# Three of six pairs and three of four batch rows close in the last work unit instead of one unit ahead of it

## The chip, the cores and the metric

The kernel runs on one core of one Trainium2 chip. The metric is the device time of one execution in microseconds (us); lower is better. All arithmetic is in 32-bit floats.

## The reference, cut to what matters

For eight batch rows of 512 tokens with 256 features the reference computes a mixture of eight experts and a shared one, and adds the input:

```
g = einsum('bsd,edf->ebsf', x, Wg);  u = einsum('bsd,edf->ebsf', x, Wu)      # 8 experts, F = 1024
expert = einsum('be,ebsd->bsd', gates, einsum('ebsf,efd->ebsd', silu(g) * u, Wd))
shared = (silu(x @ Sg) * (x @ Su)) @ Sd
out = x + (1 - sg) * expert + sg * shared        # sg: one number for each batch row
```

The kernel treats the shared expert as a ninth, with its factor `sg`.

## The kernel before

**Units.** The nine experts, two groups of four 128-wide blocks of F, and two halves of the batch (four rows each) make 36 units, done one after another. In a unit, `i` is a block of F, `j` a batch row, and `h_[i, j]` is the 128x512 tile `silu(gate) * up * coefficient`. There are 16 of them. `gate_up` makes them; `down` multiplies the 16 tiles of a unit by the weights Wd while the next unit's `gate_up` runs. In the written order of a unit, G is one step of `gate_up`, D one step of `down`, X one step of `tail`.

**Pairs.** Off the diagonal, the tiles `h_[i, j]` and `h_[j, i]` are made as one of six pairs, `PAIRS = ((1, 0), (0, 2), (3, 0), (1, 2), (3, 1), (3, 2))`. For each pair and each of gate (m = 0) and up (m = 1), three products are made where four would be needed: `R1_step` (L537) makes one that both tiles share, and `R_step` (L547) one for each. VectorE (DVE) puts D on them (L542, L552), ScalarE (ACT) applies Silu (L477), DVE multiplies (L482). ACT copies a start value into each PSUM bank ahead of it (L532).

**Down.** The same device is used again: a pair costs three 128x512 products, `r` and `s` (or `S`, which is carried in a running sum) and one of `X = h_[j, i] - h_[i, j]` (L674). Each batch row then costs two, `q` on a sum over column tiles and `b` on a sum over row tiles. These feature sums, `rows` and `cols`, are made on GpSimd (POOL) one 128x512 addition at a time (L577), and the weight forms of a pair, `ad`, `a2`, `ud` and `wd`, on POOL too (L408 to L462). So 6 x 3 + 4 x 2 = 26 products replace the 32 that a plain product of 16 tiles with two halves of Wd would take.

**Running sums.** Over the units of a batch half the results gather in SBUF tiles `accb`, `accB`, `accV`, `accS`, written by `put`, `carried` and `seeded`. `closes(u)` says in which unit a pair's V and S sums are resolved into `accb` and `accB` of its two rows, with DVE operations L605, L603, L678 and L607. A row's product `b` starts from `accb` copied by ACT into its bank (L615), so it waits for the last pair of that row.

**The end before.** The second last unit (8_0) closes all pairs and rows. The last unit (8_1) has no pairs below: `tail` makes 16 tiles x two token halves, each two 128x256 products in place of one 128x512 (L770). The closed sums are turned on DVE (L739), stored to a DRAM tile in 128-byte pieces (`endrows`, L953, eight stores a row), loaded back in row order (`endin`, L757, two loads a row), added to x on POOL (L761), and last a DVE addition puts the tail on (L779) and a store writes the output (L781). All these stores and loads are on SyncE's queue (SP), in its written order.

**What sets the order.** TensorE (PE) and POOL run in the order in which the program text records them (`manual_schedule`); the other queues get an order from a scheduler, with `issue_after` adding order where it is written. Every engine works in its own order, so an instruction that waits holds all behind it on its engine.

Of the kernel before, what the change touches and what calls it, by code (L numbers as in the profile page):

```python
# [17 lines left out]
def kernel(  # L18
# [46 lines left out]
    CI = (0.0, 1.0, -1.0, 2.0)  # L65
    PAIRS = ((1, 0), (0, 2), (3, 0), (1, 2), (3, 1), (3, 2))

    OWN = (0, 1, 2, 3)
# [405 lines left out]
    def finish(u, m, i, j, bank):  # L474
        if m == 0:
            s = spool.tile([P, S], F32, tag="sg", name=f"sg{i}{j}_{u.name}")
            nc.scalar.activation(s, bank, AF.Silu)  # L477
            u.sg[i, j] = s
        else:
            b = NI * u.h + j  # L480
            t = hpool.tile([P, S], F32, tag="h", name=f"h{i}{j}_{u.name}")
            made = ve.scalar_tensor_tensor(  # L482
                t, u.sg[i, j], coef[:, u.e, b : b + 1], bank, ALU.mult, ALU.mult
            )
            if i == j:
                first_order(u, made, "h", i)
            u.h_[i, j] = t
# [68 lines left out]
    def h_sums(u, p):  # L556


        i, j = PAIRS[p]
        if u.n + 1 == len(units):  # L560
            return
        u.X[p] = tpool.tile([P, S], F32, tag="t", name=f"X{p}_{u.name}")
        made = (gp if closes(u) and p in (1, 2, 3, 4) else ve).tensor_tensor(  # L563
            u.X[p], u.h_[j, i], u.h_[i, j], ALU.subtract
        )
        first_order(u, made, "X", p)
        for k, l in ((i, j), (j, i)):
            for which, n in (("rows", k), ("cols", l)):
                u.sums.append((which, n, (k, l)))
# [12 lines left out]

    def closes(u):

        return u.n + (2 if u.h + 1 == NH else 1) == len(units) * (u.h + 1) // NH

    def down(u, acc):
# [54 lines left out]
        def pair(p):  # L642
# [8 lines left out]
            def second():  # L651
                args = u.Wd[p][j], u.h_[j, i]
                if p in OWN and not closes(u):
                    carried(("S", p), *args)
                    return
                if p in OWN:
                    o, full = seeded(("S", p), *args)
                    if not full:
                        ve.tensor_add(o, o, acc["S", p])
                else:  # L660
                    o, _ = single(("s", p), *args)
                put(("B", i), o, -1.0)
                put(("V", p), o, -1.0)

            if closes(u) and p < SWAPPED:
                second()
                yield
                A, k = first()
            else:
                A, k = first()  # L670
                yield
                second()
# [3 lines left out]
            )  # L676
            if closes(u):
                ve.tensor_add(A, A, acc["V", p])  # L678
                put(("b", i), A, 1.0 / d)
                put(("b", j), A, -1.0 / d)  # L680
            else:
                put(("V", p), A, 1.0)
# [4 lines left out]
        done = {}  # L687
        for what in (0, 1, 2, 3, 4, "p0", "q0", 5, "q1", "p1", "q2", "p2", "q3", "p3"):
            if isinstance(what, int):
# [14 lines left out]
            else:  # L704
# [3 lines left out]
                done[what] = po  # L708
            if closes(u) and f"p{i}" in done and f"q{i}" in done:
                if CI[i] != 0.0:  # L710
                    put(("B", i), done[f"p{i}"], -CI[i])
                for r in (0, 1):
                    ends[u.h, i, r] = acc["bB"[r], i]
# [4 lines left out]
    def turn_back(h, i, r):  # L718

        if i not in backs:  # L720
            backs[i] = iopool.tile([P, S // 32, 2, 32], F32, tag="io", name=f"to{h}_{i}")
        t = backs[i]
        ve.transpose(t[:, :, r], ends.pop((h, i, r)).rearrange("p (c d) -> p c d", d=32))
        if (i, 1 - r) not in BACK[BACK.index((i, r)):]:
            for q in range(4):
                outgoing.append((squares(out, NI * h + i, q), t[ts(q, 32)]))

    last_rows = {}
    tails = {}
    ended = {}  # L730
    end_rows = {}

    def end_step(kind, i):

        b = NI * (NH - 1) + i
        if kind == "turn":
            t = iopool.tile([P, 2, S], F32, tag="io", name=f"end{i}")
            for r in range(2):
                ve.transpose(t[:, r], ends.pop((NH - 1, i, r)))  # L739
            ended[i] = t  # L740
        elif kind == "store":
            to = end_rows[i] = dram.tile([S, D], F32, tag=f"end{i}", name=f"endrows{i}")
            at = to.rearrange("(c r t) d -> r t c d", r=32, t=NT)
            for r in range(2):
                for q in range(4):
                    outgoing.append((
                        at[:, :, :, ts(4 * r + q, 32)],
                        ended[i][ts(q, 32), r].rearrange("r (t c d) -> r t c d", t=NT, d=32),
                    ))
        elif kind == "x":  # L750
            last_rows[i] = load_rows(xpool, "x", b)
        elif kind == "load":
            at = end_rows[i].rearrange("(p t) d -> p t d", t=NT)
            end_rows[i] = []
            for c in range(2):
                t = sumpool.tile([P, 2, D], F32, tag="sum", name=f"endin{i}_{c}")
                nc.sync.dma_start(t, at[:, 2 * c : 2 * c + 2])  # L757
                end_rows[i].append(t)
# [4 lines left out]
    def tail(u, i, j, c):  # L763

        first = (j, c) not in tails
        if first:
            pool, tag = (ps_g, f"g{c}") if j == 2 else (ps_o, f"po{c}")
            tails[j, c] = pool.tile([P, 2, D], F32, tag=tag, name=f"tail{j}_{c}")
# [6 lines left out]
    def store_rows(j, c):  # L775
        b = NI * (NH - 1) + j
        xr = last_rows[j][c]
        for t in (0, 1) if j == NI - 1 and c == 1 else (slice(0, 2),):
            ve.tensor_add(xr[:, t], tails[j, c][:, t], xr[:, t])  # L779
            at = out[b].rearrange("(p c t) d -> p c t d", c=2, t=2)[:, c]  # L780
            nc.sync.dma_start(at[:, t], xr[:, t])  # L781

# [8 lines left out]
    def gate_up(u, nxt):  # L791
# [5 lines left out]
        def sums(p):  # L797
            x_sums(u, p)
            w_sums(u, p)

        for p, make in ((0, w_difference), (0, w_sums), (1, w_difference), (1, w_sums)):
            make(u, p)
        if u.n:
            make_at(u, 3)
        w_difference(u, 2)
        ahead = ((0, x_difference), (0, x_sums), (1, x_difference), (1, x_sums), (2, x_difference))
        if u.n:
# [3 lines left out]
        for kind, i, m in hub_steps(u):  # L811
# [17 lines left out]
            at = range(10, 16) if u.n in LATE_FORMS else range(3, 14, 2)  # L829
            if step == at[0] - 1 and u.n and nxt is not None:  # L830
                make_ad(u)
            if step in at and u.n and nxt is not None:
                d_forms(u, at.index(step))
            yield
        if u.n == 0:
            make_ad(u)
            for p in range(len(PAIRS)):
                d_forms(u, p)
        for p in range(len(PAIRS)):
            last = p + 1 == len(PAIRS)  # L840
            if p + 3 < len(PAIRS):
                (differences if u.n else partial(w_difference, u))(p + 3)
            if nxt is not None:
                if p >= 2:
                    load_w(nxt, p - 2)
                    if p < 5:
                        make_at(nxt, p - 2)
            store_forms(u)
            if p == 5 and nxt is not None:
                load_d(nxt)  # L850
            if not last and u.n:
                seed(u, p + 1)
            for m in range(2):
                if not last and (u.n or p or m):
                    R1_step(u, p + 1, m)
                elif last and nxt is not None:
# [3 lines left out]
                for r in range(2):  # L860
                    R_step(u, p, m, r)
                    if m == 1 and r == 1:
                        h_sums(u, p)
                        if u.n == 0 and p + 2 < len(PAIRS):
                            seed(u, p + 2)
                        if p + 2 < len(PAIRS):
                            sums(p + 2)
                        if u.n == 0 and p < 2:
# [8 lines left out]
    FIRST = "TGGTGGTGG" + "G" * 16 + BLOCK * 5  # L877
    LAST = HUB + BLOCK + "GGXGGXGGX" * 5 + "X" * 17
    TAILS = [
        tuple(int(n) for n in what)  # L880
        for what in (
            "000 100 001 101 200 201 300 301 110 111 010 011 210 211 310 311 "
            "220 020 120 221 021 121 330 030 130 331 031 131 320 321 230 231"
        ).split()
    ]
    END_STEPS = {
        7: (("turn", 0), ("store", 0)), 16: (("turn", 1), ("store", 1)), 18: (("x", 0),),
        20: (("turn", 2), ("store", 2), ("x", 1)), 22: (("load", 0), ("x", 2)),
        24: (("turn", 3), ("store", 3), ("x", 3)), 28: (("add", 0),), 30: (("load", 1),),
        34: (("add", 1),), 37: (("load", 2),), 40: (("add", 2),), 44: (("load", 3),),  # L890
        47: (("add", 3),),
    }

    for i in range(NI):
# [37 lines left out]
    for u in units:  # L932
# [6 lines left out]
        for what in FIRST if u.n == 0 else LAST if nxt is None else ORDER:  # L939
            if what == "G":  # L940
                if nG == TAKE:
                    for _ in behind:
                        pass
                    if u.opens:
                        acc = {}
                    behind = down(u, acc) if nxt is not None else iter(())
                if final and nxt is not None and nG in (18, 21, 24, 27):
                    load_x(u.h + 1, (nG - 18) // 3)
                if nxt is None:
                    for what_, i in END_STEPS.get(nG, ()):  # L950
                        end_step(what_, i)
                if outgoing:
                    nc.sync.dma_start(*outgoing.pop(0))  # L953
                if nG > TAKE and nG % 2 == 0 and u.sums:
                    add_sum(u)
# [5 lines left out]
            elif what == "T":  # L961
                for _ in range(2):
                    next(turning, None)
            elif what == "X":
                i, j, c = TAILS.pop(0)
                tail(u, i, j, c)
# [56 lines left out]
```

## Time and profile before

| what | us |
|---|---|
| time, median of three runs (lowest, highest) | 2434.99 (2433.91, 2435.68) |
| the profiled execution's own time | 2433.26 |
| its span, first to last instruction | 2431.5 |
| PE busy, share of the span | 2425.3 (100%) |
| POOL busy | 2085.3 (86%) |
| DVE busy | 1918.3 (79%) |
| ACT busy | 1240.0 (51%) |
| mean granted TensorE clock | 1.000 of full speed |

A row of the timeline gives the start, the duration, the engine, the program line, the operation, out<-in, and in brackets the idle time ahead of it with what ended it. A 128x512 product shows as two records; from the start of one product to the next takes 0.86 us, and two token halves of a tail step (x2 records of 128x256 each, four in all) take the same 0.86 us. That is called a slot in what follows. 2431.5 is a span; 1.8 us lie around it in the profiled execution.

### The profile page before, as it was taken

Reading aid. Unit: us, or ns where it says so; the run is one execution under the profiler, and the core shown is the slowest. Engines: PE = TensorE matmul, PEld = TensorE weight load, DVE = VectorE, ACT = ScalarE, POOL = GpSimd, SP = SyncE. Lnnn points to the kernel's source line nnn. Section 1 sums busy time; section 2 is a strip of 40 time slices with the busy share of each in tenths; the row PEclk is TensorE's granted clock in tenths of the full one; section 3 lists DMA queues with packets and bytes.
Section 4 is the critical chain, followed back from the end, with each engine's and each line's share of the span. In section 5 each row is a group of like instructions: output and inputs, shape, how many; then the busy total and the mean of one; then the engine's idle time right before and its main releaser. Section 6 shows DMA issues by size and latency. Waiting matters only on the chain.

```text
span 2431.5 us, 22779 instructions
## 1 busy us (share of the span) xinstructions
PE 2425.3 (100%) x5736; PEld 1085.0 (45%) x5736; DVE 1918.3 (79%) x2861; ACT 1240.0 (51%) x2294; POOL 2085.3 (86%) x2321
## 2 busy tenths in 40 slices
PE   9999999999999999999999999999999999999999
PEld 4444444444444444444444444444444444444446
DVE  7788878778787877787887777777877777777795
ACT  5555454554555555555455555555455555555542
POOL 8988888898988989898888888888888888888882
PEclk9999999999999999999999999999999999999999
DMA  4333333334333333334353323323333333233245
GB/s 150 114 110 111 107 95 103 119 117 125 105 120 105 101 113 94 109 113 124 119 122 112 91 83 91 92 87 90 100 104 104 95 99 91 87 89 93 83 133 140
DMA packets 221201, 257.92 MB, mean 106 GB/s; under 512 B 64016, under 2 KB 156432, under 8 KB 221072
## 3 DMA queue, kind: packets, MB, share of 16 engines
q1 hardware_dynamic: 220240, 256.17, 35.7%
q8 instruction: 48, 0.79, 0.1%
q14 instruction: 81, 0.66, 0.1%
q10 hardware_dynamic: 832, 0.30, 0.0%
HBM read 238.59 MB, written 17.83 MB: 105 GB/s over the span
## 4 chain that ended last, share of the span: by engine, by line
PE 99%; DVE 1%; issue 0%; ACT 0%; DVEq 0%
PE c L547 30%; PE c L537 15%; PE c L515 10%; PE c L493 10%; PE r L639 7%; PE r L674 7%; PE b L616 5%; PE S L616 5%; PE q L639 5%; PE s L639 2%; PE tail L770 1%; PE B L616 0%; DVE h L482 0%; DVE c L542 0%; DVE c L552 0%
## 5 line engine op out<-in xcount | busy, mean ns | idle before, releaser
L547 PE MATMUL c<-b,wb 128*128 128x512 f32 x1728 | 847.2, 592 | 0.0
L477 ACT ACTIVATE sg<-c 128x512 f32<-128x512 f32 x576 | 343.8, 597 | 574.4 <-DVE c L552 332.4
L482 DVE SCALAR_TENSOR_TENSOR h<-sg,coef,c 128x512 f32<-128x512 f32 x576 | 427.4, 742 | 242.2 <-PE c L547 134.8
L547 PEld LDWEIGHTS c<-b,wb 128*128 128x128 f32 x1728 | 328.2, 190 | 409.2 <-issue 388.7
L537 PE MATMUL c<-v,u 128*128 128x512 f32 x864 | 441.1, 593 | 0.8 <-ACT c L532 0.8
L577 POOL TENSOR_TENSOR rows<-rows,h 128x512 f32<-128x512 f32 x280 | 369.3, 1319 | 0.0
L542 DVE TENSOR_TENSOR c<-D,c 128x512 f32<-128x512 f32 x432 | 298.7, 692 | 78.1 <-ACT sg L477 59.3
L577 POOL TENSOR_TENSOR cols<-cols,h 128x512 f32<-128x512 f32 x280 | 358.4, 1280 | 0.0
L552 DVE TENSOR_TENSOR c<-c,D 128x512 f32<-128x512 f32 x432 | 298.5, 691 | 21.2 <-PE c L547 20.7
L493 PE MATMUL c<-x,w 128*128 128x512 f32 x572 | 274.5, 592 | 0.0
L429 POOL TENSOR_TENSOR wb<-u,wb 128x256 f32<-128x256 f32 x108 | 78.8, 730 | 221.4 <-ACT wb L427 221.4
L537 PEld LDWEIGHTS c<-v,u 128*128 128x128 f32 x864 | 163.4, 190 | 207.9 <-issue 167.7
L674 PE MATMUL r<-X,ud 128*128 128x512 f32 x420 | 214.5, 592 | 0.0
L639 PE MATMUL r<-h,wd 128*128 128x512 f32 x420 | 214.5, 592 | 0.0
L515 PE MATMUL c<-x,at 128*128 128x512 f32 x432 | 208.5, 592 | 0.0
L525 ACT COPY D<-c 128x512 f32<-128x512 f32 x284 | 165.7, 584 | 81.4 <-DVE h L482 81.3
L563 DVE TENSOR_TENSOR X<-h,h 128x512 f32<-128x512 f32 x202 | 198.1, 981 | 6.8
L577 POOL TENSOR_TENSOR rows<-h,h 128x512 f32<-128x512 f32 x140 | 195.1, 1394 | 0.0
L577 POOL TENSOR_TENSOR cols<-h,h 128x512 f32<-128x512 f32 x140 | 180.6, 1290 | 0.0
L499 ACT COPY P<-c 128x512 f32<-128x512 f32 x216 | 126.4, 587 | 106.1 <-PE c L493 101.5
L493 PEld LDWEIGHTS c<-x,w 128*128 128x128 f32 x572 | 108.5, 190 | 135.9 <-issue 111.7
L615 ACT COPY S<-accS 128x512 f32<-128x512 f32 x132 | 77.8, 590 | 157.5 <-DVE accV L603 140.7
(115 smaller groups left out, 3473.6 us busy)
## 6 DMA issues: line engine op xcount, KB each, us to landing
b<-xs SPq DMA_DIRECT2D x210, 512.0 KB, 3.6
v<-xs SPq DMA_DIRECT2D x210, 256.0 KB, 2.6
wd<-in_L_cond_Wd_dram SPq DMA_DIRECT2D x32, 512.0 KB, 4.9
w<-in_L_cond_Wg_dram SPq DMA_DIRECT2D x127, 128.0 KB, 3.5
w<-in_L_cond_Wu_dram SPq DMA_DIRECT2D x127, 128.0 KB, 3.6
f<-xd SPq DMA_DIRECT2D x12, 512.0 KB, 5.2
xs<-f SPq DMA_DIRECT2D x18, 256.0 KB, 2.9
xin<-in_x_dram SPq DMA_DIRECT2D x16, 256.0 KB, 4.4
```

The source lines that it names most:

```text
L477: nc.scalar.activation(s, bank, AF.Silu)
L482: made = ve.scalar_tensor_tensor(t, u.sg[i, j], coef[:, u.e, b : b + 1], bank, ALU.mult, ALU.mult)
L493: nc.tensor.matmul(bank, u.raw[i][:, m, 0], xhub[u.h, i][:, 0], start=True, stop=True)
L515: nc.tensor.matmul(bank, u.at[i][:, m], xhub[u.h, i][:, 1], start=False, stop=True, skip_group_check=True,)
L537: nc.tensor.matmul(bank, u.U[p][:, m], u.V[p], start=False, stop=True, skip_group_check=True)
L542: first_order(u, ve.tensor_sub(other, u.Ds[j, m], bank), "other", p, m)
L547: nc.tensor.matmul(bank, u.W[p][:, r, m], u.VB[p][:, r], start=False, stop=True, skip_group_check=True,)
L552: ve.tensor_add(bank, bank, u.Ds[j, m])
L577: gp.tensor_tensor(sums[n], u.h_[n, n] if first else sums[n], u.h_[at], ALU.add)
L616: nc.tensor.matmul(po, w, b, start=not full, stop=True, skip_group_check=full)
L639: nc.tensor.matmul(po, w, b, start=True, stop=True)
L674: nc.tensor.matmul(A, u.Ud[p], u.X[p], start=False, stop=True, skip_group_check=True)
```

## The change

The last unit now keeps pairs 0, 1 and 3 (those among rows 0, 1 and 2) in pair form with feature sums, and closes them and the rows 0, 1 and 2. Pairs 2, 4 and 5, which touch row 3, and row 3 itself still close one unit ahead. In the last unit, every tile with row 3 or block 3 goes through `tail`: seven tiles, 14 steps. The order of the pairs in that unit becomes 0, 1, 3, 2, 4, 5. The DRAM loop of row 3 stays in the middle of the unit; that of rows 0, 1 and 2 moves to its end, with six of row 2's eight stores on ACT's queue, held behind ACT's last Silu by `issue_after`.

```diff
+    LAST_PAIRS = (0, 1, 3)
+    LAST_ROWS = (0, 1, 2)
...
-        if u.n + 1 == len(units):
+        if p not in pairs_of(u):
             return
         u.X[p] = tpool.tile([P, S], F32, tag="t", name=f"X{p}_{u.name}")
-        made = (gp if closes(u) and p in (1, 2, 3, 4) else ve).tensor_tensor(
+        made = (gp if closes(u, p) and p in (1, 2, 3, 4) else ve).tensor_tensor(
...
-    def closes(u):
-
-        return u.n + (2 if u.h + 1 == NH else 1) == len(units) * (u.h + 1) // NH
+    def is_last(u):
+
+        return u.n + 1 == len(units)
+
+    def pairs_of(u):
+
+        return LAST_PAIRS if is_last(u) else range(len(PAIRS))
+
+    def closes(u, p=None, i=None):
+
+        if u.h + 1 < NH:
+            return u.closes
+        if (p in LAST_PAIRS) if i is None else (i in LAST_ROWS):
+            return is_last(u)
+        return u.n + 2 == len(units)
...
-        for what in (0, 1, 2, 3, 4, "p0", "q0", 5, "q1", "p1", "q2", "p2", "q3", "p3"):
+        order = (0, 1, 2, 3, 4, "p0", "q0", 5, "q1", "p1", "q2", "p2", "q3", "p3")
+        for what in (0, 1, "p0", "q0", 3, "q1", "p1", "q2", "p2") if is_last(u) else order:
...
+    def send():
+
+        queue, i, to, at = outgoing.pop(0)
+        made = queue.dma_start(to, at)
+        if i is not None:
+            closing_stores.setdefault((i, queue), []).append(made)
...
+                    queue = nc.scalar if i == 2 and 4 * r + q < 6 else nc.sync
...
-            if step == at[0] - 1 and u.n and nxt is not None:
+            if step == at[0] - 1 and u.n:
                 make_ad(u)
-            if step in at and u.n and nxt is not None:
-                d_forms(u, at.index(step))
+            if step in at and u.n and order[at.index(step)] in pairs_of(u):
+                d_forms(u, order[at.index(step)])
...
-    LAST = HUB + BLOCK + "GGXGGXGGX" * 5 + "X" * 17
+    LAST = HUB + BLOCK * 3 + "GDGDGGDGDGD" + "GDDGDDGGGG" + "GGGXGGGXX" + "X" * 11
     TAILS = [
...
-            "000 100 001 101 200 201 300 301 110 111 010 011 210 211 310 311 "
-            "220 020 120 221 021 121 330 030 130 331 031 131 320 321 230 231"
+            "330 331 030 031 300 301 310 311 130 131 230 231 320 321"
...
     END_STEPS = {
...
+        24: (("turn", 3), ("store", 3), ("x", 3)), 34: (("load", 3),),
+        39: (("turn", 0), ("store", 0)), 42: (("turn", 1), ("store", 1)),
+        43: (("turn", 2), ("store", 2), ("load", 0)), 46: (("add", 3), ("add", 0)),
     }
+    LAST_STEPS = (("load", 1), ("load", 2), ("add", 1), ("add", 2))
...
-                    behind = down(u, acc) if nxt is not None else iter(())
+                    behind = down(u, acc)
...
+                    for made in closing_stores[2, nc.scalar]:
+                        issue_after(made, u.last_silu)
+                    for made in closing_stores[2, nc.sync]:
+                        issue_after(made, *closing_stores[1, nc.sync])
+                    for what_, i in LAST_STEPS:
+                        end_step(what_, i)
```

## The prediction

> **What bounds the kernel now.** I read the page first (busy shares, the chain that ended last), then the timeline of the last 80 us, where the change lies, and last the landing times of the DRAM loop.
>
> ```profile
> span 2431.5 us, 22779 instructions
> ...
> PE 2425.3 (100%) x5736; PEld 1085.0 (45%) x5736; DVE 1918.3 (79%) x2861; ACT 1240.0 (51%) x2294; POOL 2085.3 (86%) x2321
> ...
> PE 99%; DVE 1%; issue 0%; ACT 0%; DVEq 0%
> ```
>
> PE never stops: a slot saved there is time saved, and a slot in which PE waits is time lost. The end is one block of tail products, one addition, one store:
>
> ```profile
> 2410.35 0.60 ACT L477 ACTIVATE sg<-c 128x512 f32<-128x512 f32 x1 [1.86 <-DVE c L552]
> ...
> 2411.99 15.70 PE L770 MATMUL tail<-wd,h 128*128 128x256 f32 x72
> ...
> 2427.80 0.76 DVE L779 TENSOR_TENSOR xin<-tail,xin 128x256 f32<-128x256 f32 x2 [0.17 <-PE tail L770]
> ```
>
> The DRAM loop is over long before: POOL adds the last `endin` at 2405.98 to 2408.5, 19 us ahead of DVE's last addition. POOL has been ahead of PE too:
>
> ```profile
> 2354.18 1.27 POOL L577 TENSOR_TENSOR cols<-cols,h 128x512 f32<-128x512 f32 x1
> ...
> 2361.56 1.27 POOL L577 TENSOR_TENSOR cols<-cols,h 128x512 f32<-128x512 f32 x1
> ...
> 2375.76 0.73 POOL L429 TENSOR_TENSOR wb<-u,wb 128x256 f32<-128x256 f32 x1 [9.76 <-ACT wb L427]
> ```
>
> ```profile
> 2367.03 1.02 PE L639 MATMUL q<-cols,ad 128*128 128x512 f32 x2
> ```
>
> The addition at 2361.56 is the last of row 2's column sum; the product at 2367.03 uses it, 4.2 us after it is done. How long a row's closing takes is seen once, in unit 8_0:
>
> ```profile
> 2360.29 0.70 DVE L678 TENSOR_TENSOR r<-r,accV 128x512 f32<-128x512 f32 x1
> ...
> 2361.75 1.28 DVE L607 SCALAR_TENSOR_TENSOR accb<-r,accb 128x512 f32<-128x512 f32 x2
> ```
>
> ```profile
> 2363.07 0.59 ACT L615 COPY b<-accb 128x512 f32<-128x512 f32 x1 [2.12 <-DVE accb L607]
> ```
>
> ACT starts 0.04 us after DVE ends; the X product of that pair ended at 2360.25, and its row's `b` product starts at 2364.38, so 4 us lie between, filled by other products. The DRAM loop, tile `endrows`:
>
> ```profile
> L953 SPq DMA_DIRECT2D endrows<-end x32: 569/616/773, 2352.3 to 2399.5; - x32
> L757 SPq DMA_DIRECT2D endin<-endrows x8: 326/404/603, 2365.6 to 2402.8; - x8
> ...
> DMA to landing us min/median/max: 2.1/3.2/4.7
> ```
>
> Looked at by stretches, stores land 2.1 to 4.1 us after issue, loads 3.0 to 4.7.
>
> **The change part by part.** *Taken away:* 32 tail slots become 14, and 3 x 3 + 3 x 2 = 15 products are added: three slots fewer, 3 x 0.86 = **-2.6 us**. This holds only if PE never waits.
>
> *Moved and added.* POOL gains in unit 8_1 four `ad` (0.455 us each in the groups by shape), one `a2` (0.63), three `ud` (0.46), three `wd` (0.735), 12 sums (1.28) and two X, and loses two X in 8_0: some 21 us. It idles about 29 us between 2360 and 2412 (busy 8.1, 9.4 and 5.4 us in the three stretches), so the sum fits; what matters is where it stands. DVE gains 12 operations net, ACT copies for the carried S sums and three rows. All engines keep a fixed order, so I followed that order for the last two units: each instruction starts when the one ahead on its engine is done and what it waits for is done plus 0.04 us, with the duration or back-to-back spacing of its row (DVE 0.60 and 0.69, with h 0.66 and 0.74; ACT 0.51 and 0.59; POOL 1.23 and 0.69). The same walk over the old order lands within 0.4 us of the trace's starts. PE's new waits:
>
> 1. *q of row 2, unit 8_0.* The new weight forms stand in POOL's order ahead of the sum above: 4 x 0.455 + 0.63 + 3 x 0.46 + 3 x 0.735 = 6.04 us against 4.2 us of slack: **1.85 us**.
> 2. *b of row 0, unit 8_1,* only two slots behind pair 1's X product, on which `accb0` depends. After the last up product of pair 3, DVE's order has the addition, a subtraction and h (0.60 + 0.60 + 0.66), then L678 0.69 and `accb0` 0.68, then ACT's copy 0.59, with five hops 0.2: 4.02 us. PE has two products between, 1.72 less 0.16 of drain: **2.46 us**.
> 3. *b of row 1,* two slots behind pair 3's X: L678 0.61, an h 0.66, two L607 (0.61 + 0.685, the sign is given with the second), ACT 0.59, hops 0.12 = 3.28, less 1.56: **1.75 us** with rounding.
> 4. *b of row 2,* whose bank ACT must first empty of row 1 (0.59), behind a Silu (0.51), and refill (0.59): **0.48 us**.
> 5. Five short ones, S of pair 3 and s of pair 4 in 8_0 (ACT now evicts S; DVE makes two X that POOL made, 0.98 each), X of pairs 0 and 3, and the start value of pair 2's bank: 0.37 + 0.19 + 0.35 + 0.24 + 0.46 = **1.6 us**.
>
> Together 8.15, less the 0.15 us gap that the trace has ahead of 2368.04: 8.0. PE ends 8.0 - 2.6 = **5.4 us later**, at about 2433.1 in the trace's time.
>
> *The finish.* Row 2's `b` is now evicted just before pair 5's products, and its loop runs in the open. Pair 5's last Silu starts at about 2420.5 (its gate product is at 2377.59 + 38 x 0.86 = 2410.2 without waits, 2418.2 with them, 1.02 to its end, DVE 0.7 behind others). ACT then issues six stores, 0.66 us each (SP's row 0.62 with its gap): the third at 2422.4. SP's last store of row 2 must wait for that one's landing, since the eight DMA semaphores are used in turn; with 2.9 us it starts at 2425.3 and lands at 2428.2. The `endin` loads of row 1 stand behind it on SP (2426.0), those of row 2 wait for all stores (2428.3 and 2428.7) and land 3.5 us later, 2431.8 and 2432.2. POOL is still adding row 1 (two of 1.23 us from 2429.6), then adds row 2 from 2432.0 to 2434.5; DVE's last additions start at 2434.6, the last store at 2435.6. Before, it was issued at 2428.7: **+6.9 us**. Nothing stands behind ACT's six stores; behind SP's waiting one stand also row 0's output stores, which have time. The `b` tiles of pairs 4 and 5, loaded behind `endrows` stores of rows 3 and 0, still land some 8 us before use. Seven output stores that were spread over 14 us now leave in 6, close to the 320 GB/s that the windows show at 2427 to 2430; I add 0.3. **Sum: +7.2 us**, a span of 2438.7, 2440.5 in the profiled execution; the median of the runs stands 1.7 us above it: **2442.2**.
>
> *A rule and the row.* The Trainium skill, "DMA: Bandwidth & Descriptors", section "Anatomy of one DMA", gives about 2.0 us and bytes over 436 GB/s for a DMA (stated for GpSimd's path): 2.15 us for a 64 KB store, 2.6 for a 256 KB load. The trace shows 2.1 to 4.1 and 3.0 to 4.7. By the rule the two stores and one load of the chain take 2.4 us less than mine, the loop hides behind PE, and the sum is +5.4; I take rows from the middle. Against the change speaks "TensorE: Matmul & The Clock Gate", section "What's actually happening": the clock halves after an idle window of about 3.4 us. This trace shows 1.000 throughout and no such gap; my longest wait is 2.5 us, so I add nothing. If it fell, 14 tail slots at half speed would cost up to 12 us more.
>
> **The rivals.** *PE ends last* (17 in 100): quick landings hide the loop; +5.4, 2440.4, from 2439.5 to 2441. *Slow loop* (20): landings near 4.1 and 4.7 make it +9 to +11: 2444 to 2446. *Waits half covered* (8): POOL or DVE run ahead of my walk, waits of 4 us in all, +1 to +4: 2436 to 2439.8. *Faster* (2): PE doesn't wait in the last unit. The three slots decide once waits 1 to 5 sum to under 2.6 us: with none and the loop hidden, 2432.4. Against it stands the dependence of `b` of row 0 on a product two slots ahead. That the change does nothing is excluded: the orders differ on every engine.
>
> **How the numbers follow.** The likeliest case, PE's waits and then the DRAM loop at middling landings, has 53 in 100, +6 to +9. A measurement tells about 0.2% (4.9 us) from no change. Slower by more: 53 + 20 + most of 17 = 86; within: 12; faster: 2. The range leaves out the half-covered case, the fast one and the slowest loops: 2439.2 to 2446.0.
>
> **What would show it.** PE idle about 8 us in the last 70, releasers ACT `b` (2.5 and 1.8 us) and POOL `cols` (1.9); DVE's last L779 waiting on POOL, not on PE; POOL's `xin` waiting on `endin`; the chain of waits ending in POOL and DMA. Wrong would be: PE idle under 4 us; DVE's last additions released by PE (the loop hidden); a lower clock in the tail; store landings on ACT's queue unlike SP's.

## The result and the profile after

The changed kernel takes 2447.3 us (median of five runs, 2443.2 to 2450.3), against 2434.99 us before: 1.0045 times as long, with a 95% interval of 1.0034 to 1.0057. A second set of five runs, measured later, gave 2445.55 against 2435.49 us, 1.0041 (1.0028 to 1.0054). The forecast was 2442.2 us with a range of 2439.2 to 2446.0. The direction is as forecast; the first median lies 1.3 us above the range, the second inside it.

The profiled run took 2447.3 us with a span of 2445.5. From its page, the rows that answer to those shown of the kernel before:

```profile
span 2445.5 us, 22738 instructions
...
PE 2428.0 (99%) x5694; PEld 1078.0 (44%) x5694; DVE 1928.0 (79%) x2873; ACT 1246.2 (51%) x2306; POOL 2105.2 (86%) x2344
...
PE 95%; POOL 2%; DVE 2%; DMA 1%; issue 1%; ACT 0%; ACTq 0%; POOLq 0%; SPq 0%; DVEq 0%
```

PE has 42 records fewer and is yet busy 2.7 us longer. That is the first sign that idle time is not all: some products took longer. The view of PE's waits over the last 146 us (what waited, for what, us in total, times, the longest):

```profile
PE b L631 <- ACT b L630: 4.2, 3, 2.4
PE q L654 <- POOL cols L580: 1.9, 1, 1.9
PE r L689 <- ACT sg L480: 1.0, 1, 1.0
PE S L631 <- ACT S L630: 0.9, 1, 0.9
PE r L689 <- DVE accB L618: 0.2, 1, 0.2
```

These are the waits that the forecast named, in the places that it named. In the kernel before this view is empty. The timeline around the first of the two long ones (start, duration, engine and line; in brackets the idle time ahead and its releaser):

```profile
2371.68 1.26 POOL L580 TENSOR_TENSOR cols<-cols,h 128x512 f32<-128x512 f32 x1
...
2373.00 1.55 PE L654 MATMUL q<-cols,ad 128*128 128x512 f32 x2 [1.87 <-POOL cols L580]
...
2374.34 1.91 PE L540 MATMUL c<-v,u 128*128 128x512 f32 x2
...
2376.05 1.49 PE L550 MATMUL c<-b,wb 128*128 128x512 f32 x2
...
2377.38 1.02 PE L631 MATMUL b<-rows,wd 128*128 128x512 f32 x2
```

The wait is 1.87 us (forecast 1.85). But the products behind it follow each other at 1.34, 1.71 and 1.33 us instead of 0.86, for 3.4 us. Cut at the changes of the granted clock, the table of stretches says why. Its columns are the stretch, its length, then the busy time and number of instructions of PE, weight load, DVE, ACT and POOL, then the granted clock, the DMA share and GB/s:

```profile
2370.15:2373.57 3.42, 1.55 (x5) 0.48 (x5) 2.25 (x4) 3.13 (x6) 3.34 (x5) 1.00 0.47 145
2373.57:2376.98 3.41, 3.41 (x6) 1.35 (x5) 0.69 (x1) 0.07 (x1) 2.50 (x3) 0.50 0.16 58
2400.87:2404.29 3.42, 1.06 (x4) 0.33 (x3) 2.68 (x5) 1.18 (x2) 3.42 (x5) 1.00 0.82 293
2404.29:2407.70 3.41, 3.41 (x6) 1.34 (x5) 0.76 (x2) 1.77 (x3) 3.41 (x4) 0.50 0.00 0
2414.53:2417.94 3.41, 1.87 (x6) 0.56 (x4) 3.23 (x6) 1.18 (x2) 3.34 (x4) 1.00 1.03 221
```

Twice a stretch of 3.41 us ran at half clock: right after the stretch with the wait for q of row 2 (PE busy 1.55 of 3.42 us), and right after the one with the wait for b of row 0 (1.06 us). Behind the wait for b of row 1 (1.87 us busy) there was none. The two half-clock stretches begin 30.72 us apart, nine times 3.413: they lie on one fixed grid. In the kernel before no such stretch stands ahead of the end of PE's last product.

The finish, from the timeline:

```profile
2428.49 0.60 ACT L480 ACTIVATE sg<-c 128x512 f32<-128x512 f32 x1 [1.35 <-DVE c L555]
2428.49 4.07 ACTq L755 DMA_DIRECT2D endrows<-end  x6
...
2429.77 11.39 PE L806 MATMUL tail<-wd,h 128*128 128x256 f32 x52
...
2432.82 2.67 SPq L788 DMA_DIRECT2D endin<-endrows  x4
...
2436.52 4.95 POOL L797 TENSOR_TENSOR xin<-xin,endin 128x512 f32<-128x512 f32 x4 [12.38 <-DMA endin<-endrows]
...
2439.05 3.21 DVE L815 TENSOR_TENSOR xin<-tail,xin 128x512 f32<-128x512 f32 x6 [0.53 <-POOL xin L797]
```

As forecast, POOL waits for the DRAM loop and DVE for POOL. (In this trace POOL waits for row 1's load, which stands on SP behind row 2's last store; row 2's additions follow without a gap.) But DVE ends at 2442.26, and PE alone would have let it end at 2442.0: PE's last record starts at 2440.78, and in the kernel before DVE ended 1.24 us after the start of that record. So the loop is 0.2 us late, not 1.5.

**Where the 14.0 us between the two spans went.** The first 200 us, whose code is the same in both, took 2.4 us more in this profile. From 2300 us on I add up by how much the starts of PE's neighbouring instructions lie further apart than their 0.43 us: 14.4 us in this trace, 0.65 before. Of the difference of 13.7 us, 3.4 lie in the two half-clock stretches and 10.3 in waits. The three slots give back 2.6. The finish takes 0.6 (the loop 0.2, the last stores the rest). 2.4 + 10.3 + 3.4 - 2.6 + 0.6 = 14.1.

### The profile page after: what moved, and what is told of

It is laid out like the page before. It is cut to its first block, busy times and chain, and to the rows that moved or that the text cites. A ratio compares the mean times of both kernels' runs of the same rounds, so it can differ in the third digit from the quotient of the medians.

```text
span 2445.5 us, 22738 instructions
## 1 busy us (share of the span) xinstructions
PE 2428.0 (99%) x5694; PEld 1078.0 (44%) x5694; DVE 1928.0 (79%) x2873; ACT 1246.2 (51%) x2306; POOL 2105.2 (86%) x2344
## 4 chain that ended last, share of the span: by engine, by line
PE 95%; POOL 2%; DVE 2%; DMA 1%; issue 1%; ACT 0%; ACTq 0%; POOLq 0%; SPq 0%; DVEq 0%
PE c L550 29%; PE c L540 15%; PE c L518 10%; PE c L496 10%; PE r L654 7%; PE r L689 7%; PE b L631 5%; PE S L631 5%; PE q L654 5%; PE s L654 2%; DVE h L485 0%; POOL cols L580 0%; POOL rows L580 0%; DMA xin<-in_x_dram 0%; DVE c L555 0%
```

## The experiments

Theory A was formed from this: a wait costs its idle time, and besides 1.7 us (half of 3.41) if it leaves PE idle for more than about half of one of the grid's windows. Below, "gaps" is the sum just described, from 2300 us on; PE then ends by gaps - 0.65 - 2.6 later than in the kernel before. It is the better measure here, because the start differs by 0 to 4 us between profiles of the same code, and the medians can move with it. For one such start, in the kernel called forms_late below:

```profile
56.87:60.28 3.41, 3.41 (x5) 1.35 (x6) 2.40 (x3) 1.71 (x4) 3.41 (x3) 0.50 0.70 234
```

and the same stretch in the kernel before, whose start of course has waits as well:

```profile
56.87:60.28 3.41, 3.41 (x9) 1.52 (x8) 2.56 (x4) 2.25 (x5) 3.41 (x4) 1.00 0.86 255
```

| kernel | median, us | ratio to before (95%) | gaps, us | half-clock stretches from 2300 us on |
|---|---|---|---|---|
| changed | 2447.3 | 1.0045 (1.0034 to 1.0057) | 14.4 | 2 |
| again | 2445.55 | 1.0041 (1.0028 to 1.0054) | 14.4 | 2 |
| fill | 2442.59 | 1.0033 (1.0020 to 1.0045) | 7.6 + 3.4 | 0 |
| forms_late | 2445.6 | 1.0041 (1.0029 to 1.0054) | 11.0 | 1 |
| fill_sp | 2443.34 | 1.0032 (1.0021 to 1.0044) | 7.6 + 3.4 | 0 |
| x_pool | 2445.1 | 1.0036 (1.0023 to 1.0048) | 9.4 | 0 |
| b_added | 2445.0 | 1.0034 (1.0023 to 1.0046) | 9.2 | 0 |
| all_mended | 2442.04 | 1.0020 (1.0011 to 1.0029) | 6.65 | 0 |
| x_pool_right | 2440.25 | 1.0021 (1.0012 to 1.0030) | 6.8 | 0 |
| all_right | 2438.53 | 1.0012 (1.0003 to 1.0020) | 3.8 | 0 |

(The 3.4 us of fill are its four idle products. Before: 2435.0 to 2436.1 beside them.)

**again.** The changed kernel, unaltered.

> The changed kernel once more, for its spread and a second trace. Theory A (PE's waits cost twice: as idle time, and as a stretch of 3.41 us at half clock whenever a wait leaves PE idle for more than about half of one of the chip's clock windows): the waits for q of row 2 and b of row 0 last 1.9 and 2.4 us as before, but how many half-clock stretches follow depends on where the windows lie: 0 to 3 of them, 1.7 us each, so runs spread over 5 us and more (2443 to 2450), with the longer ones at a lower mean clock. Rival B (the waits alone cost, and the two half-clock stretches of the first trace are an accident of that run): runs within 2.5 us, as for the kernel before, and no stretch at half clock in the new trace.

Five runs from 2443.4 to 2446.45: less spread than the first five, and less than the 5 us that theory A expected. The trace has the same waits to 0.02 us and again two half-clock stretches, again each right behind the windows with PE busy 1.53 and 1.04 of 3.41 us. So they are no accident of one run; rival B falls. That the runs differ by the number of stretches is not shown: the start takes part in it.

**fill.** Two products that nothing reads, in the place of each of the two long waits.

```
+            if is_last(u) and key == ("b", 0):
+                for _ in range(2):
+                    nc.tensor.matmul(po, w, b, start=True, stop=True)
             if full:
                 nc.scalar.copy(po, acc[key])
...
+            if u.n + 2 == len(units) and key == ("q", 2):
+                for _ in range(2):
+                    nc.tensor.matmul(po, u.ad[1], u.cols[1], start=True, stop=True)
             nc.tensor.matmul(po, w, b, start=True, stop=True)
```

> The changed kernel, with two idle products put into the same accumulator bank ahead of q of row 2 and two ahead of b of row 0; the product that follows overwrites them, so what is computed stays the same. PE is busy in the time in which it waited. Theory A: both waits shrink to under 0.9 us, the order ends at most 0.4 us later by them, and no half-clock stretch follows: 2 x 1.7 = 3.4 us less than a run with two stretches, so a median of about 2444 against 2447.3, runs within 3 us, mean clock 1.000. Rival B (waits alone): the time stays where it is or grows by 0.3, 2447.5. Rival C (the DRAM loop of row 2 sets the end): half-clock stretches gone, but the time goes down by less than 1 us.

```profile
2370.92 1.12 PE L660 MATMUL q<-cols,ad 128*128 128x512 f32 x2 [0.17 <-POOL cols L580]
...
2400.01 1.13 PE L634 MATMUL b<-rows,wd 128*128 128x512 f32 x2 [0.68 <-ACT b L633]
```

The products start no earlier in the order than before, only the idle time ahead of them is filled, and both half-clock stretches are gone. The median falls by 3.0 us beside "again", to 2442.59; the runs lie within 2.3 us. Theory A expected 3.4 less and about 2444. With the two waits kept in length and the clock taken out, the kernel takes 7.1 us more than before.

**forms_late.** The last unit makes its weight forms as late as three others do, and like them adds two feature sums a step instead of one.

```
-    LATE_FORMS = (1, len(units) // NH, len(units) // NH + 1)
+    LATE_FORMS = (1, len(units) // NH, len(units) // NH + 1, len(units) - 1)
```

> The changed kernel, but the last unit makes its weight forms six steps later on POOL and adds two feature sums a step instead of one, as two other units do: the sums of unit 8_0 no longer stand behind the new forms. Theory A: the wait of 1.87 us for q of row 2 is gone, about 0.5 us of it comes back at pair 2's first product in the last unit, and one of the two half-clock stretches goes with it: 1.4 + 1.7 = 3.1 us less, about 2444.2. Rival B (waits alone): 1.4 us less, 2445.9. Rival D (the new forms only sit where POOL is idle anyway): no change.

The wait for q of row 2 is gone, 0.26 us of it comes back at an up product of the last unit, and there is one half-clock stretch instead of two, behind b of row 0. The gaps fall from 14.4 to 11.0 us: 3.4 less, against 3.1 expected. The median shows nothing of it (2445.6 against 2445.55): in its profile the start took 4.0 us more than in that of the kernel before, 1.7 of it the half-clock stretch shown above. By the gaps theory A holds; the median alone would have spoken for rival D.

**gaps.** The kernel before, with eleven waits put in.

```
+    GAPS = {2: 2, 3: 3, 4: 4, 5: 2, 6: 3, 7: 4, 10: 2, 11: 3, 12: 4, 13: 2, 14: 3, 15: 4}
...
+            n = GAPS.get(u.n, 0) if key == ("q", 1) else 0
+            if n:
+                nc.tensor.matmul(po, w, b, start=True, stop=True)
+                for _ in range(n):
+                    nc.scalar.copy(po, po)
             nc.tensor.matmul(po, w, b, start=True, stop=True)
```

(Unit 6 has no product of this kind, so eleven waits.)

> The kernel before with waits put in on purpose, to measure the disputed cost by itself: in eleven of the middle units q of row 1 is multiplied once more into its bank, ScalarE then copies that bank onto itself two, three or four times, and the right product waits for it (and overwrites it, so the result is the same). From the rows of the trace the waits are 1.5 us (four), 2.1 us (three) and 2.7 us (four): 23 us of waiting and 9.4 us of products, +32.4 us. Theory A (a window of 3.41 us in which PE is idle for more than about 1.7 us is followed by one at half clock): none behind the waits of 1.5 us, about 2 of 3 behind those of 2.1, 3 of 4 behind those of 2.7, so some 5 stretches of 1.7 us: +41 us, 2476. Rival E (only a window without any product throttles, as the Trainium skill's rule of an idle window reads): no stretch, +32.4 us, 2467.4.

The waits came out 0.2 us shorter: 1.26 us four times, 1.86 three times, 2.46 or 2.47 four times. Behind those of 1.26 us no half-clock stretch followed, behind those of 1.86 one of three, behind those of 2.47 four of four: five stretches, as theory A expected, where rival E expected none. Four of the windows with a wait and what follows each, cut on the grid that the stretches give (columns as above):

```profile
292.29:295.70 3.41, 1.55 (x5) 0.64 (x4) 3.05 (x6) 1.71 (x3) 3.33 (x5) 1.00 0.00 0
295.70:299.12 3.42, 3.42 (x6) 1.38 (x5) 1.39 (x2) 0.08 (x1) 3.34 (x5) 0.50 0.20 77
...
848.66:852.07 3.41, 1.85 (x5) 0.90 (x6) 2.38 (x4) 1.44 (x3) 3.33 (x4) 1.00 0.00 0
852.07:855.49 3.42, 3.42 (x10) 1.51 (x9) 1.30 (x3) 2.39 (x5) 3.26 (x6) 1.00 0.00 0
...
916.93:920.34 3.41, 1.36 (x4) 0.30 (x2) 3.36 (x6) 2.06 (x5) 3.33 (x5) 1.00 0.00 0
920.34:923.75 3.41, 2.99 (x4) 1.45 (x5) 0.69 (x1) 0.52 (x2) 3.33 (x5) 0.50 0.00 0
...
435.65:439.06 3.41, 2.15 (x6) 0.79 (x5) 2.98 (x6) 1.14 (x2) 3.33 (x4) 1.00 0.00 0
439.06:442.47 3.41, 3.41 (x9) 1.52 (x8) 2.05 (x4) 1.70 (x4) 3.33 (x5) 1.00 0.00 0
```

The waits in the windows from 292.29 and from 848.66 are both 1.86 us long. The first lies whole in one window, the other is cut by a border (1.56 us in this window, 0.30 in the one before); only the first is paid for twice. The median is 39.7 us over before. The sum is 20.5 us of waits (the view of waits), 0.26 us of restart at each, 9.4 of products and 5 x 1.7 of clock, 41.3; without the clock it is 32.8.

**fill_sp.** Fill, and row 2's stores all on SP.

```
-                    queue = nc.scalar if i == 2 and 4 * r + q < 6 else nc.sync
+                    queue = nc.sync
...
-                    for made in closing_stores[2, nc.scalar]:
+                    for made in []:
                         issue_after(made, u.last_silu)
```

> The kernel with the idle products (fill), and besides all eight row-2 stores of the DRAM loop on SP, none on ScalarE behind the last Silu. It tells what the open loop is worth, without half-clock stretches in the way. The prediction's finish (POOL's additions of row 2 end 1.5 us after PE's last product allows, 0.3 for the pile of stores): 1.5 to 1.8 us less than fill, DVE's last additions released by PE. Reading of fill's trace (the last addition starts 0.6 us later than PE alone would let it): 0.6 us less. Rival F (SP's queue is the bound, and stores moved there are late as well): no less, DVE's last additions still released by POOL.

DVE's last additions are still released by POOL, as rival F expected, though after 0.34 us of idle time instead of 0.54 (it is 0.17 where PE releases them). They end 0.2 us later than PE alone would let them, against 0.6 in fill. But the two traces of the changed kernel differ by as much (0.2 and 0.7), and the medians don't tell fill and fill_sp apart (2443.34 against 2442.59). So the open loop is worth 0.2 to 0.7 us here and not the 1.5 to 1.8 of the forecast; whether SP's queue serves row 2 better is not shown.

**x_pool.** Meant to move two X to POOL, on top of forms_late; the edit hit other units, as the units are numbered to 35.

```
-        made = (gp if closes(u, p) and p in (1, 2, 3, 4) else ve).tensor_tensor(
+        made = (gp if closes(u, p) and p in (1, 2, 3, 4) or (u.n, p) in ((16, 3), (17, 0)) else ve).tensor_tensor(
```

> The kernel with the late weight forms (forms_late), and besides X of pair 3 in unit 8_0 and X of pair 0 in the last unit made by POOL, as the kernel before had the first. Theory P (these two took 1.68 and 1.80 us on DVE where the prediction put 0.98, since POOL read two tiles from SBUF at the same time; DVE's delay is what PE waited for): PE's waits for S of pair 3 (0.90) and X of pair 0 (0.97) fall to under 0.4 us each, and from the first wait in unit 8_0 to the last tail product PE needs 1.0 to 2.0 us less than in forms_late. Rival Q (ScalarE's start values set these waits, as the profile's releasers name them): both waits stay within 0.2 us.

So this run says nothing of theory P: both waits and both slow X are there as before. What it did was to move two X in the middle of the program, and there it cost 1.0 us: PE's products start 3.8 us behind those of the kernel before from 200 to 1160 us and 4.8 from 1200 to 2290, with one wait between, for a sum on POOL:

```profile
1165.59 1.13 PE L654 MATMUL q<-cols,ad 128*128 128x512 f32 x2 [0.72 <-POOL cols L580]
```

(The 1.6 us in the expectation of all_right compares DVE's instructions by their number; two of them had moved to POOL.) The run says something of the clock, though: the wait for b of row 0 is 2.36 us again, but a window's border cuts it, and no stretch at half clock follows:

```profile
2398.15:2401.57 3.42, 2.37 (x6) 0.76 (x4) 3.35 (x6) 0.98 (x2) 3.42 (x4) 1.00 0.43 140
2401.57:2404.98 3.41, 2.09 (x5) 1.06 (x6) 1.49 (x3) 1.52 (x3) 3.41 (x4) 1.00 0.48 167
2404.98:2408.39 3.41, 3.41 (x9) 1.52 (x8) 2.95 (x6) 1.42 (x4) 3.41 (x4) 1.00 0.33 57
```

**b_added.** The changed kernel; b of the last unit no longer starts from the sum so far.

```
-            full = key in acc and not turned[k]
+            full = key in acc and not turned[k] and not (is_last(u) and key[0] == "b")
```

> The changed kernel, but in the last unit ScalarE does not put the sum so far into the bank ahead of the b products of rows 0, 1 and 2; the product starts the bank afresh and DVE adds it to the sum behind it. The same is computed, PE no longer waits for a sum that needs the X product two slots ahead. Theory A: the waits of 2.4, 1.5 and 0.3 us on ScalarE go, about 2 us of short ones on DVE's reads of the banks come in their place, none of them over 1.2 us, so no half-clock stretch follows b of row 0; that of q stays: 2.2 + 1.7 = 3.9 us less than the changed kernel with two stretches, 2442 to 2443. Rival G (the bank, not the sum, is late): waits of the same sizes on DVE in their place, and the stretch stays.

The waits of 2.36, 1.54 and 0.32 us on ACT give way to 0.62, 0.92 and 1.09 us on DVE, and no stretch follows b of row 0: rival G falls. The stretch behind q didn't come either, although its wait is 1.86 us; the window with most of it, and the next:

```profile
2370.92:2374.33 3.41, 1.68 (x4) 0.30 (x2) 2.95 (x5) 3.11 (x6) 3.33 (x4) 1.00 0.45 129
2374.33:2377.75 3.42, 3.29 (x8) 1.61 (x9) 0.69 (x1) 1.16 (x3) 3.21 (x4) 1.00 0.29 107
```

PE was busy for 1.68 us in it, and this was enough; 1.55 us was not. The gaps fall by 5.2 us (3.9 expected, with the stretch of q still there), of which the time can't gain all, as the loop now ends 1.35 us later than PE alone would let it; the median of 2445.0 again has a late start in it (3.9 us in the profile).

**all_mended.** Late forms, the additions of b and of S of pair 3 on DVE, row 2's stores on SP, and the two misplaced X.

```
-            full = key in acc and not turned[k]
+            full = key in acc and not turned[k] and not (is_last(u) and key[0] == "b") and not (u.n + 2 == len(units) and key == ("S", 3))
```

> The causes undone together: late weight forms, the two X on POOL, b of the last unit and S of pair 3 in unit 8_0 added by DVE instead of put into the bank ahead, and row 2's stores all on SP. Theory A: what is left are short waits of PE, each under 1.3 us and with 0.26 us of restart, so no half-clock stretch, 4 to 6 us in all against 2.6 us saved by three slots, and the loop nearly hidden: 1 to 4 us over the kernel before, about 2437.5. Rival H (something else in the change costs: the longer list of stores, the extra work on DVE and POOL): still 6 us or more over the kernel before. Rival I (the three slots come through): 1 to 2 us under the kernel before.

6.0 us over the kernel before (2442.04 against 2436.07), where theory A expected 1 to 4: a miss, and rival H had asked for 6 or more. The profile's span is 4.9 us over: 0.4 by the start, 1.0 by the two X in the middle, and by the gaps PE ends 3.4 us later. The loop is hidden, DVE's last additions are released by PE. So the profile speaks for A and the median doesn't; all_right below decides. The gaps are 6.65 us, above the 4 to 6 expected, as X of pair 0 was still on DVE.

**x_pool_right.** Forms_late with the two X where they were meant.

```
+        made = (gp if closes(u, p) and p in (1, 2, 3, 4) or (len(units) - u.n, p) in ((2, 3), (1, 0)) else ve).tensor_tensor(
```

> The move of two X to POOL made where it was meant: the units are counted 0 to 35, and the run before this one had moved X of units 16 and 17, in the first half, so that the two X in question stayed on DVE (1.68 and 1.80 us again, the same two waits). Here X of pair 3 in unit 34 and X of pair 0 in unit 35 go to POOL, with the late weight forms as there. Theory P (what PE waits for is DVE, held up by an X that takes twice its time while POOL reads SBUF too): the waits for S of pair 3 (0.90) and for X of pair 0 (0.97) fall to under 0.4 us each, 1.0 to 2.0 us less of PE's gaps from unit 34 on than in forms_late (8.0 us without its half-clock stretch... 9.4 us in the run with the X misplaced). Rival Q (ScalarE's start values set these waits, as the profile's releasers name them): both waits stay within 0.2 us.

Pair 3 of unit 8_0 in the timeline of the changed kernel:

```profile
2336.45 1.27 POOL L580 TENSOR_TENSOR rows<-h,h 128x512 f32<-128x512 f32 x1
2336.60 1.68 DVE L566 TENSOR_TENSOR X<-h,h 128x512 f32<-128x512 f32 x1
...
2338.20 0.68 DVE L622 SCALAR_TENSOR_TENSOR accb<-r,accb 128x512 f32<-128x512 f32 x1
...
2338.91 0.59 ACT L630 COPY S<-accS 128x512 f32<-128x512 f32 x1 [1.71 <-DVE accb L622]
...
2339.55 1.13 PE L631 MATMUL S<-h,wd 128*128 128x512 f32 x2 [0.90 <-ACT S L630]
```

The same in the timeline of this one:

```profile
2337.40 1.28 DVE L622 SCALAR_TENSOR_TENSOR accb<-r,accb 128x512 f32<-128x512 f32 x2
...
2337.63 1.28 POOL L566 TENSOR_TENSOR X<-h,h 128x512 f32<-128x512 f32 x1 [1.10 <-PE c L550]
...
2338.72 0.59 ACT L630 COPY S<-accS 128x512 f32<-128x512 f32 x1
...
2339.90 1.02 PE L631 MATMUL S<-h,wd 128*128 128x512 f32 x2
```

In the first, X starts 0.15 us behind POOL's sum and lasts until 0.56 us after the sum's end; an X beside an idle POOL takes 0.69 us, so little of it was done while POOL's sum ran. The release of the bank that ACT needs for S stands behind it on DVE. With X on POOL, S waits for nothing, and the wait for X of pair 0 is gone too. The gaps are 6.8 us, 2.6 less than in x_pool, which had the same waits otherwise and no half-clock stretch either (1 to 2 expected). Rival Q falls: ACT is named as releaser, but DVE was late.

All 205 X on DVE in the changed kernel's trace show the same rule. The 62 that began with POOL idle, or within 0.2 us of the end of its operation, took 0.69 us. The 143 that began with more than 0.2 us of a POOL operation still to run ended 0.55 us after that operation (0.546 to 0.555), whatever was left of it, up to 1.26 us.

**all_right.** All causes undone, the X at the right place, and the last products of rows 1 and 2 further apart.

```
-    LAST = HUB + BLOCK * 3 + "GDGDGGDGDGD" + "GDDGDDGGGG" + "GGGXGGGXX" + "X" * 11
+    LAST = HUB + BLOCK * 3 + "GDGDGGDGDGDGDDGGDDGGG" + "GGGXGGGXX" + "X" * 11
...
-        43: (("turn", 2), ("store", 2), ("load", 0)), 46: (("add", 3), ("add", 0)),
+        44: (("turn", 2), ("store", 2), ("load", 0)), 46: (("add", 3), ("add", 0)),
```

> The causes undone together, with the two X at the right place, and the products of rows 1 and 2 moved one or two slots apart in the written order of the last unit. From the trace of the run with all mended (PE's gaps from unit 34 on 6.65 us): less 1.2 for X of pair 0, less 0.5 for S of pair 3, less 1.1 for the last up product behind DVE, so 3.9 us of gaps against 0.65 before and 2.6 us saved: PE ends 0.6 us later than in the kernel before, the loop 0.5 to 1 us behind it, and the 1.6 us that the misplaced X cost in the middle are gone. Theory A: 0 to 2.5 us over the kernel before, same within 0.2%. Rival H (something else in the change costs): 5 us or more over it. Rival I (the three slots come through): 1 to 2 us under it.

The gaps are 3.8 us (3.9 expected), so PE ends 0.6 us later than before. The median is 3.3 us over the kernel before, 1.0012 times (1.0003 to 1.0020): within the 0.2%, under the 5 us that rival H asked for, and a little over the 2.5 us expected, because the loop is in the open again:

```profile
2418.25 11.39 PE L806 MATMUL tail<-wd,h 128*128 128x256 f32 x52
...
2428.78 2.49 POOL L797 TENSOR_TENSOR xin<-xin,endin 128x512 f32<-128x512 f32 x2 [0.67 <-DMA endin<-endrows]
2431.31 0.76 DVE L815 TENSOR_TENSOR xin<-tail,xin 128x256 f32<-128x256 f32 x2 [0.53 <-POOL xin L797]
```

PE's last product is done at 2429.5; the last additions start at 2431.3, 1.6 us after PE alone would let them. No version tried beats the kernel before. The reserve of three slots is there, but waits of 3.2 us (3.8 less the 0.65 of before) take it up again, and row 2's loop stands behind.

## Why the prediction was right in direction and short in size

*Three slots saved, -2.6 us: right.* In all_right PE ends 0.6 us later, by gaps of 3.2 us more and the three slots less.

*PE's five groups of waits: the right places, 2.3 us too small in sum.* Measured from start to start of the neighbouring products, less 0.86 for each product:

| wait | forecast | measured |
|---|---|---|
| q of row 2 | 1.85 | 2.13 |
| b of row 0 | 2.46 | 2.60 |
| b of row 1 | 1.75 | 1.80 |
| b of row 2 | 0.48 | 0.58 |
| S of pair 3 | 0.37 | 1.16 |
| X of pair 0 | 0.35 | 1.23 |
| s of pair 4, X of pair 3, start value | 0.89 | 1.00 |
| sum | 8.15 | 10.5 |

Two things are in the difference. The term "DVE makes two X that POOL made, 0.98 each" was mis-sized: 0.98 is the mean of a row whose members run from 0.69 to 1.80 us. The two that mattered took 1.68 and 1.80 us, each begun together with a sum on POOL, and so S of pair 3 and X of pair 0 came 1.7 us later than forecast. Two corrections to the forecast's own words belong here: the X of unit 8_0 that went from POOL to DVE is that of pair 3 (and of pair 1), while X of pair 0 in the last unit is a new one. The Trainium skill has this, "SBUF — State Buffer", section "Who interferes with whom": an addition or subtraction on VectorE with both inputs in SBUF contends with GpSimd's reads. This case agrees: of the 1.68 us 1.12 passed until POOL's sum was over, and the 143 X above ended 0.55 us after POOL. Most of the rest, some 0.1 us at a wait, is a slower first product: 0.97 us to the next start instead of 0.86.

*"My longest wait is 2.5 us, so I add nothing": this step failed.* The forecast read the skill's clock gate ("TensorE: Matmul & The Clock Gate", section "What's actually happening") as asking for a window of 3.4 us without any product. The same section says that the windows run free, and the traces confirm that, with 3.413 us and one grid for the whole program. What decides is PE's busy time in one window, and it need not be zero. In all these traces there are 21 windows, from 200 us on and ahead of PE's end, in which PE was idle for 1.2 us or more: the ten with 1.86 us or more (up to 2.47) were each followed by one at half clock, the eleven with 1.73 us or less were not. The change therefore paid for the waits of 1.87 and 2.36 us a second time: 3.4 us, all of which fill gave back. The forecast's other bound, 14 tail slots at half speed, didn't come about: a stretch lasts one window and ends when that window was busy.

*The finish: the right chain, too large.* DRAM loop, POOL, DVE, in this order, as forecast; the landings were near the forecast too (in the changed kernel's last 36 us, medians of 2.2 us for the stores on ACT's queue, 2.8 on SP's, 3.5 for the loads, against 2.9 and 3.5). SP's last store of row 2 started at 2432.08, when the third store on ACT's queue had landed, also as forecast. What was too large is the time of the loop. PE ended 12.7 us after the start of the last Silu, where the forecast has 12.6 (2420.5 to 2433.1), so PE's side came out as forecast. POOL was done 13.0 us after that start, where the forecast has 14.0 (2434.5), and DVE ended 0.8 us behind POOL, where it has DVE's last store 1.1 us behind. The third store was issued 1.4 us after the Silu's start, not 1.9, and landed in 2.2 us, not 2.9. In the second trace of the changed kernel and in that of fill, PE's 12.7 us is the same, POOL needs 13.4 and 13.3, and the loop is 0.7 and 0.6 us late.

*The sum.* Forecast +7.2: 8.0 - 2.6 + 1.5 + 0.3. Measured, without the start: 10.3 + 3.4 - 2.6 + 0.6 = 11.7. In the first set of runs the median rose by 12.3 us, in the second by 10.1. That the second median lies inside the range is partly luck: its upper end was left for a slow DRAM loop, which did not come, and about 1 us too much at the finish stood against 2.3 us of waits and 3.4 us of clock too little. That fill's median (+7.1) agrees with the forecast is luck too: with the start taken out its profile is 9.0 us longer than that of the kernel before, whose own start was an early one.

*The rivals.* "PE ends last", "slow loop" and "waits half covered" all fell: the loop was the last by 0.2 us (0.7 in the second trace), landings were ordinary, and no wait was covered.

## What to carry to other kernels

A saved PE slot is worth 0.86 us; a wait of 2 us in its place costs 2, and 1.7 more where it empties half a clock window, so in a kernel whose PE never stops, two waits of 1.2 us, each in a window of its own, are cheaper than one of 2.4; several waits in one window were not tried. Before an operation with two SBUF inputs is moved to DVE, look at what POOL does at that moment, and count 0.55 us from the end of POOL's operation, not the mean of the row; and when the releaser named is an eviction on ACT, look at what freed that eviction. Where the start of a program differs by several us from run to run, add up PE's gaps in the stretch concerned, and don't judge an edit of 3 us by its median.

## What the runs showed of the hardware

The clock falls to half for exactly one window of 3.413 us after a window in which PE was busy for 1.55 us or less, and not after one in which it was busy for 1.68 us or more; the same wait of 2.36 us cost 1.7 us more or nothing, depending on whether a window's border cut it. A 128x512 subtraction on DVE with both inputs in SBUF took 0.69 us with POOL idle, and with more than 0.2 us of a POOL operation still to run it ended 0.55 us after that operation (143 of 143 in one trace). A wait costs PE about 0.26 us more than the profile shows in brackets: 0.16 us at its front, which the modelled end of the product before covers, and 0.1 us in the first product behind it.
